# Four image layers on one core: depthwise filters cut into pieces of sixteen rows, two additions moved to VectorE, and a new planner clock

## The chip, the cores and the metric

The kernel runs on one core of a Trainium2 chip. A core has five engines that work side by side, each through its own queue of instructions in a fixed order: TensorE (PE in the profile, its weight loads PEld), VectorE (DVE), ScalarE (ACT), GpSimd (POOL), and SyncE (SP), which here issues all the DMAs. Engines wait for each other through semaphores. The metric is the time on the device in microseconds. Before the change it is 5206.15 us, the median of three runs from 5203.51 to 5209.27.

## What is computed

The input is 32 images of 56x56 pixels and 96 channels, in float32. Four layers follow each other:

```
layer 0: w = sigmoid(mean(x) @ Wr + br)              # four experts, mixed per image
         h = relu(bn(x @ sum_e w_e Wpw_e))           # 96 -> 384 channels
         h = relu(bn(depthwise3x3(h, sum_e w_e Wdw_e)))
         x = x + bn(h @ sum_e w_e Wpwl_e)            # 384 -> 96, residual
layer 1: x = x + depthwise5x5(x, kernel)
layer 2: x = bn(depthwise3x3(relu(x), dw) @ pw)      # 96 -> 96
layer 3: shifted-window attention (7x7 windows, 3 heads) with its residual,
         then x + gelu(layernorm(x) @ w1 + b1) @ w2 + b2
```

## The kernel before

**Stages and pipeline.** The work of an image is split into four stages, written as Python generators: `stage_router` (the mean and the mixed weights of layer 0), `stage_conditional` (the rest of layer 0), `stage_depthwise` (layers 1 and 2) and `stage_swin` (layer 3). In each step of the outer loop, four images are in the pipeline, each in another stage.

**Who sets the order.** The stages don't issue instructions. They record them with a `Recorder` (`chip`), with what each reads and writes. `order()` then plays the whole recording against a simple clock: `cost()` says how long each instruction holds its engine, `TO_TENSOR` and `CROSSING` how long a result takes to reach another engine, `PLAN` when each stage should begin and how long it should last in units of an image. Of the instructions that are ready, each engine takes the one that is due first. The result is a fixed list for every engine, which `give` writes out; all traced lines are therefore L500, and one goes by the names of tiles. Where this clock finds TensorE idle for over `SPARE_AFTER` = 250 ns, it inserts a filler matmul of the identity with itself (`banks<-ident 128x128`), whose result nobody uses. On the chip the lists are executed in this order, whatever the planner's clock said.

**Layer 0.** The image lies as channels by pixels in `xT`. In strips of 14 rows and blocks of 128 hidden channels, TensorE expands (`banks<-xT,wmix`), ACT writes the relu, and the 3x3 depthwise filter is one scaling on ACT and eight VectorE instructions (`h<-h,mix,h`, 128x784). The projection back (`project`) is three matmuls for seven rows (`banks<-h,wmix`), eight such groups in an image. ACT then writes scale times sum plus bias into `y`, and POOL adds `y` to `xT` (`add`).

**Layers 1 and 2.** The two depthwise filters run on TensorE as small matmuls of 32x32. The image is copied by DMA from `xT` into `x1`, where a partition holds one channel and one of four neighbouring rows (`RB` = 4), and the free dimension 14 blocks of four rows and the columns. A matmul takes 32 partitions (8 channels, 4 rows) and a banded matrix (`band5`, `band3`); because the filter crosses from one block of four rows into the next, each column offset needs two matmuls. The function `tiles` issues a step of 3 groups x 4 tiles, twelve matmuls on different parts of the array, and accumulates 10 steps (5x5) or 6 steps (3x3) in three banks. Each half of the image has its own accumulation. The first filter's result goes through ACT (relu) into `x2`, the second's through ACT into `x3` and by DMA back to channels by pixels in `filtered`; columns are turned by three for the shifted windows. Then TensorE multiplies by `pw` into `res`.

**Layer 3.** `perceptron`, at its end, has POOL add the mean that the kernel keeps in the 97th column of `res` (`tb<-res`) and then the bias `b2` (`tb<-tb,L_conv_b`), after which VectorE adds the bank of the second linear map (`tb<-banks,tb`) and SP sends `tb` to HBM.

**SP's queue.** It holds, in one order: the load of a next image (`xT<-in_x`), the 12 copies into `x1` of each image (`x<-xT`), 36 copies to `filtered`, and 8 outputs (`out<-tb`).

Of the kernel before, what the change touches and what calls it, by code (L numbers as in the profile page):

```python
# [22 lines left out]
E = 4  # L23
# [15 lines left out]
RB = 4  # L39
NBLK = H // RB  # L40
# [47 lines left out]
def banded(k, before, back):  # L88

    w = np.zeros((NQ, 8, RB, NG, 2, k.shape[2], 8, RB), np.float32)
    for q in range(NQ):
        for g in range(NG):
            first = 32 * g + 8 * ((q - g) % NQ if back else q)
            for m in range(2):
                for row in range(RB):
                    for r in range(RB):
                        dy = RB * m + row - r - before  # L100
                        if 0 <= dy < k.shape[1]:
                            for c in range(8):
                                w[q, c, row, g, m, :, c, r] = k[first + c, dy]
    return w.reshape(P, NG, 2 * k.shape[2], 32)
# [3 lines left out]
def tile_scores_in_range(ctx: ExitStack, tc: tile.TileContext, a: dict, flag: bass.AP):  # L108
# [38 lines left out]
    ("vector", "scalar_tensor_tensor"): (150, 1.16), ("vector", "tensor_tensor"): (180, 0.96),  # L147
    ("vector", "tensor_scalar"): (190, 0.78), ("vector", "tensor_reduce"): (180, 0.95),
    ("vector", "tensor_copy"): (180, 1.1), ("vector", "reciprocal"): (180, 6.2),
    ("scalar", "activation"): (200, 0.72), ("scalar", "copy"): (200, 0.72),  # L150
    ("gpsimd", "tensor_tensor"): (200, 2.1), ("gpsimd", "memset"): (150, 0),
    ("sync", "dma_start"): (550, 0),
}
LANDING = 3000
IMAGE_LANDING = 12000

PLAN = {"router": (-0.14, 1), "conditional": (0.72, 1.14), "depthwise": (1.48, 1.13), "swin": (3.09, 0.92)}
CROSSING = 350

TO_TENSOR = {"vector": 1500, "gpsimd": 1500, "scalar": 1000, "sync": 700}  # L160
SPARE_AFTER = 250
SHARING = 1.36


def cost(engine, method, args, kw):
    if method == "preload_act_table_set":
        return 1300
    out = kw["out"] if "out" in kw else args[0]
    n = math.prod(out.shape[1:])
    if engine == "tensor":  # L170
        if method == "transpose":
            return 127
        k, m = args[1].shape[0], math.prod(args[1].shape[1:])
        if k == 32 and m == 32:
            return 68 * n / 392
        if k == 32:
            return 86
        if m == 32:
            return 75 if n < 128 else 255
        return 195 if n < 128 else 80 + 1.6 * n  # L180
    if len(args) > 3 and args[3] == ALU.pow:
        return 200 + 200 * n
    fixed, each = COST[engine, method]
    if engine == "scalar":
        if kw.get("accum_out") is not None:
            fixed += 190
        if hasattr(kw.get("scale"), "shape"):
            each += 0.37 if hasattr(kw.get("bias"), "shape") else 0.23
        elif hasattr(kw.get("bias"), "shape"):
            each += 0.25  # L190
    return fixed + each * n
# [69 lines left out]
class Recorder:  # L261
# [77 lines left out]
    def order(self):  # L339
# [15 lines left out]
        for w in self.work:  # L355
            for b in w.uses:
                b.left = len(b.users)
        queues = {e: [] for e in self.ENGINES}
# [7 lines left out]
        def available(w):  # L366
            need = {}
# [6 lines left out]

        running = {}

        def share(now):

            nonlocal count
            rate = SHARING if len(running) > 1 else 1.0  # L380
            for r in running.values():
                r["left"] -= (now - r["since"]) / r["rate"]
                r["since"], r["rate"] = now, rate
                r["end"] = free[r["work"].engine] = now + max(r["left"], 0.0) * rate
                heapq.heappush(events, (r["end"], count, r))
                count += 1
# [19 lines left out]
        def begin(w):  # L406
# [9 lines left out]
            if e == "gpsimd" or e == "vector" and w.calls[0][0] == "scalar_tensor_tensor":  # L416
                running[e] = {"work": w, "left": w.ns, "since": now, "rate": 1.0}
                share(now)
                return
            free[e] = now + w.ns  # L420
            heapq.heappush(events, (free[e], count, None))
            heapq.heappush(events, (free[e] + w.landing, count + 1, w))
# [8 lines left out]
        while left:  # L431
            for e in self.ENGINES:
                if free[e] > now:
                    continue
                held = []
                while queues[e]:
                    item = heapq.heappop(queues[e])
                    w = self.work[item[1]]
                    if not available(w):
                        held.append(item)  # L440
                        continue
                    begin(w)
                    left -= 1
                    if e == "tensor":
                        spares, begun = 0, True
                    break
                else:
                    if e == "tensor" and begun and self.spare and now >= free[e] + SPARE_AFTER and self.spare[2].free:
# [5 lines left out]
                        w.ns = cost(e, "matmul", operands, {})  # L454
# [10 lines left out]
            while events and events[0][0] <= now:  # L465
# [3 lines left out]
                elif isinstance(w, dict):  # L469

                    if w["end"] == now and running.get(w["work"].engine) is w:
                        del running[w["work"].engine]
                        w["work"].end = now
                        done(w["work"], now)
                        share(now)
# [28 lines left out]
def kernel(  # L504
# [17 lines left out]
    xTs = ring("xT", [C, H * W], 2)  # L522
# [3 lines left out]
    ys = ring("y", [C, RT], 2)  # L526
# [9 lines left out]
    x3s = ring("x3", [P, NG, NBLK // 2 + 1, W], 1)  # L536
    oTs = ring("oT", [C + 1, 2 * RT], 2)
    x1s = ring("x1", [P, NG, NBLK + 1, W + 4], 1)
# [1028 lines left out]
```

## Time and profile before

| | before |
|---|---|
| median of three runs | 5206.15 us |
| span of the profiled execution | 5212.6 us |
| time from one image to the next, middle of the run | 155.0 us |
| banded matmuls (32x32), busy in all | 856.3 us, 24576 instructions |
| VectorE taps of layer 0 (`h<-h,mix,h`), busy in all | 3309.6 us, 3072 instructions |
| POOL: `xT<-y,xT` / `tb<-res`, busy in all | 470.2 us / 477.7 us |
| VectorE's last tap to the end | 285 us |

The profiled execution is one run with the profiler on; its own time is its span, 0.12% above the median. A float32 matmul of the program appears as two instructions, so 24576 instructions are 12288 matmuls. In a list in order of time, the first number is the start in microseconds from the begin of the span, the second the length of the merged group, the last the count. "Idle before" in a group's line is idle time of that engine just before the group, with what ended it.

### The profile page before, as it was taken

What the parts mean: (1) busy time and instruction counts of PE and PEld (TensorE: products, weight loads), DVE (VectorE), ACT (ScalarE), POOL (GpSimd) and SP (SyncE); (2) the same over time, 40 slices, a digit from 0 to 9 for tenths busy, and PEclk for the clock granted to TensorE, in tenths of its full rate; (3) what the DMA queues carried; (4) which work ended last, traced back from release to release, by engine and by line L of the source; (5) the groups of instructions that cost most, each with busy time, mean ns of one, the idle gap of its engine ahead of it and who ended that gap; (6) DMA issues with size and microseconds to landing.
All of it is one profiled execution on the core that took longest, in us unless ns stands there. A gap on an engine that the chain in (4) does not pass through costs nothing.

```text
span 5212.6 us, 139630 instructions
## 1 busy us (share of the span) xinstructions
PE 5050.6 (97%) x58578; PEld 3343.9 (64%) x58578; DVE 4300.9 (83%) x5561; ACT 3836.9 (74%) x7649; POOL 3028.8 (58%) x2432
## 2 busy tenths in 40 slices
PE   5789999999999999999999999999999999999999
PEld 4556666666666666666666666666666666666677
DVE  7877988888888888888888888888888888888722
ACT  3457778877778777777877777877777877777755
POOL 5455766565665556666555665656576555566533
PEclk9899999999999999999999999999999999999999
DMA  1111101111111111111111111111111111110110
GB/s 43 23 28 37 38 18 32 33 39 36 39 21 30 31 39 36 39 23 30 33 35 37 37 30 26 30 36 38 37 35 22 32 33 39 36 39 21 23 28 19
DMA packets 482577, 166.34 MB, mean 32 GB/s; under 512 B 477951, under 2 KB 478612, under 8 KB 478868
## 3 DMA queue, kind: packets, MB, share of 16 engines
q1 hardware_dynamic: 481940, 157.33, 14.8%
q8 instruction: 463, 7.59, 0.6%
q14 instruction: 174, 1.43, 0.1%
HBM read 41.60 MB, written 38.54 MB: 15 GB/s over the span
## 4 chain that ended last, share of the span: by engine, by line
PE 74%; POOL 10%; DVE 5%; ACT 5%; issue 4%; DMA 1%; SPq 0%; ACTq 0%; DVEq 0%; POOLq 0%
PE banks L500 74%; DVE h L500 3%; POOL tb L500 3%; POOL lnd L500 2%; POOL xT L500 2%; ACT exps L500 2%; POOL exps L500 2%; POOL var L500 1%; ACT hid L500 1%; ACT h L500 1%; DMA out<-tb 1%; DVE wmix L500 1%; DVE hid L500 1%; ACT slots L500 0%; DVE res L500 0%
## 5 line engine op out<-in xcount | busy, mean ns | idle before, releaser
L500 DVE SCALAR_TENSOR_TENSOR h<-h,mix,h 128x784 f32<-128x784 f32 x3072 | 3309.6, 1113 | 71.1 <-ACT h L500 54.0
L500 POOL TENSOR_TENSOR var<-var,mhalf 112x4 f32<-112x4 f32 (+1 forms) x512 | 775.2, 1519 | 426.3 <-DVE var L500 419.6
L500 PE MATMUL banks<-x,band 32*32 32x392 f32 x24576 | 856.3, 510 | 0.0
L500 POOL TENSOR_TENSOR xT<-y,xT 96x392 f32<-96x392 f32 x256 | 470.2, 1838 | 445.5 <-ACT y L500 444.1
L500 PE MATMUL banks<-xT,wmix 96*128 96x448 f32 (+1 forms) x1536 | 697.9, 553 | 0.5 <-DVE wmix L500 0.5
L500 ACT ACTIVATE h<-h,biasd,s 128x784 f32<-128x784 f32 x384 | 398.9, 1039 | 366.1 <-DVE h L500 366.0
L500 ACT ACTIVATE hid<-banks,c 128x448 f32<-128x448 f32 (+1 forms) x768 | 436.5, 582 | 288.3 <-PE banks L500 279.9
L500 POOL TENSOR_TENSOR tb<-res 112x384 f32<-112x384 f32 (+1 forms) x256 | 476.4, 1866 | 286.7 <-DMA out<-tb 196.7
L500 PEld LDWEIGHTS banks<-w,hid 128*112 128x112 f32 x5376 | 584.7, 183 | 82.0 <-issue 37.8
L500 PE MATMUL banks<-hT,w 96*128 96x448 f32 (+1 forms) x1536 | 615.6, 502 | 0.2 <-DVE tb L500 0.2
L500 POOL TENSOR_TENSOR lnd<-res,var 112x384 f32<-112x384 f32 (+1 forms) x512 | 594.8, 1168 | 32.8 <-PE banks L500 16.2
L500 ACT ACTIVATE h<-banks,bias,s 128x448 f32<-128x448 f32 (+1 forms) x768 | 538.6, 709 | 91.0 <-PE banks L500 85.4
L500 PE MATMUL banks<-w,hid 128*112 128x96 f32 x5376 | 593.1, 267 | 7.4 <-ACT hid L500 6.4
L500 PE MATMUL banks<-h,wmix 128*96 128x392 f32 x1536 | 557.7, 501 | 15.7 <-ACT h L500 15.7
L500 PEld LDWEIGHTS banks<-x,band 32*32 32x32 f32 x24576 | 404.7, 103 | 250.9 <-issue 165.9
L500 ACT ACTIVATE exps<-banks 49x196 f32<-49x196 f32 x1536 | 506.2, 330 | 40.2 <-PE banks L500 15.3
L500 POOL TENSOR_TENSOR exps<-exps,keep_column 49x147 f32<-49x147 f32 x224 | 207.1, 925 | 480.8 <-ACT exps L500 427.4
L500 PEld LDWEIGHTS banks<-h,wmix 128*96 128x96 f32 x1536 | 244.1, 165 | 256.8 <-issue 209.2
L500 PEld LDWEIGHTS banks<-xT,wmix 96*128 96x128 f32 x1536 | 261.2, 192 | 200.7 <-issue 95.5
L500 DVE TENSOR_REDUCE var<-lnsq 112x4 f32<-112x388 f32 (+1 forms) x512 | 253.1, 497 | 157.6 <-POOL lnd L500 118.1
L500 ACT ACTIVATE h<-h,mix 128x784 f32<-128x784 f32 x384 | 364.5, 949 | 18.0 <-POOL h L500 10.1
L500 PEld LDWEIGHTS banks<-hT,w 96*128 96x128 f32 x1536 | 256.4, 190 | 144.9 <-issue 74.8
(132 smaller groups left out, 7460.2 us busy)
## 6 DMA issues: line engine op xcount, KB each, us to landing
xT<-in_x SPq DMA_DIRECT2D x32, 1176.0 KB
x<-xT SPq DMA_DIRECT2D x384, 98.0 KB
out<-tb SPq DMA_DIRECT2D x128, 168.0 KB
filtered<-x SPq DMA_DIRECT2D x384, 49.0 KB
filtered<-x SPq DMA_DIRECT2D x384, 42.0 KB
out<-tb SPq DMA_DIRECT2D x128, 126.0 KB
filtered<-x SPq DMA_DIRECT2D x384, 7.0 KB
wpw<-in_L_conv_Wpw SPq DMA_DIRECT2D x1, 576.0 KB
```

What stands on the lines that cost most here:

```text
L500: getattr(getattr(self.nc, w.engine), method)(*args, **kw)
```

## The change

*Pieces of sixteen rows.* The channels are taken in three sets of 32 (`NSET`). In `x1` a partition now holds one of two channels and one of 16 rows (`BIN`), and six overlapping pieces, ten rows apart (`BOUT`), cover the image; four channel groups lie behind each other in the free dimension. Sixteen rows in give twelve after the 5x5 filter (`BMID`) and ten after the 3x3, so a filter no longer crosses from one piece to the next. `products` issues all the matmuls of one filter of one set as one unit of the order: 5 or 3 steps of 16 matmuls with 336 columns, each step on all 16 tiles of the array, into four banks. The number of matmuls per image, 384, stays. `x1` has three buffers and `x2` two. `xT` gets zero rows above and below the image. The copies into `x1` are 48 per image, each to 8 partitions (one row number of 16); those to `filtered` are 33 per image; 6 copies of zeros (`nought`) per image clear rows of `x2` outside the image. POOL repeats three columns of `x3` instead of two ACT copies per group.

*Residual of layer 0.* The scale s3 is multiplied into the expert weights once at the start. The projection's bank is added to `xT` with the bias by one VectorE instruction; `y`, its ACT instruction and POOL's add go.

*Mean of layer 3.* POOL writes `res` + `b2` into `tb` in one instruction instead of two. VectorE adds the bank, the mean (as a scalar per partition) and `tb` in one instruction per 112 pixels, seven for each pair of chunks instead of two.

*The planner's clock.* `cost` and `COST` get other constants, TensorE's time depends on the shape of its tiles, and a change of shape costs 170 ns. Among matmuls that are due at nearly the same time, one of the shape in use goes first. VectorE and POOL instructions on SBUF alone exclude each other. `PLAN`, `TO_TENSOR` and `CROSSING` change. A DMA is taken to hold SP for 120 ns, before 550.

In the written order of the whole program, fillers go from 836 to 1508 and changes of the array's tile shape from 1808 to 1031. In the even part they are 10 and 38 fillers per image.

The diff, cut to its core:

```diff
-RB = 4
-NBLK = H // RB
+NSET = 3
+NSLOT = NSET * NQ
+BIN, BMID, BOUT = 16, 12, 10
+NBLK = -(-H // BOUT)
...
-    ("sync", "dma_start"): (550, 0),
+    ("sync", "dma_start"): (120, 0),
...
-PLAN = {"router": (-0.14, 1), "conditional": (0.72, 1.14), "depthwise": (1.48, 1.13), "swin": (3.09, 0.92)}
-CROSSING = 350
-
-TO_TENSOR = {"vector": 1500, "gpsimd": 1500, "scalar": 1000, "sync": 700}
+PLAN = {"router": (-0.041, 1.106), "conditional": (0.712, 1.09), "depthwise": (1.53, 0.85), "swin": (3.09, 0.92)}
+CROSSING = 30
+
+TO_TENSOR = {"vector": 1127, "gpsimd": 2494, "scalar": 1420, "sync": 50}
 SPARE_AFTER = 250
-SHARING = 1.36
+CHANGE = 170
+SAME = 0.0315
...
+def tensor_time(calls):
+
+    rows, columns = tiling(calls[0])
+    beside = min(len(calls), (P // rows) * (P // columns))
+    if beside == 16 and len(calls) % 16:
+        beside = 12
+    total = 30 if beside > 1 else 0
+    for method, args, kw in calls:
+        m = math.prod(args[1].shape[1:])
+        n = args[1].shape[0] if method == "transpose" else math.prod(args[2].shape[1:])
+        total += 2 * ((max(n, m) if beside == 1 else n) / 1.2 + 5) / beside
+    return total
...
-    x1s = ring("x1", [P, NG, NBLK + 1, W + 4], 1)
-    x2s = ring("x2", [P, NG, NBLK + 2, W + 2], 1)
+    x1s = ring("x1", [P, NQ, NBLK, W + 4], 3)
+    x2s = ring("x2", [P, NQ, NBLK, W + 2], 2)
...
-            y = chip.new(ys)
-            chip.scalar.activation(y, pt[:C, :RT], AF.Identity, bias=bias3, scale=s3)
-            return y
+            return pt[:C, :RT]
 
         def add(n, y):
             rows = xT[:, 7 * n * W : 7 * (n + 1) * W].part(n)
-            chip.gpsimd.tensor_tensor(rows, y, rows, ALU.add)
+            chip.vector.scalar_tensor_tensor(rows, y, bias3, rows, ALU.add, ALU.add)
...
+        for u in range(NSET):
+            x1 = chip.new(x1s)
+            for r in range(BIN):
+                chip.sync.dma_start(
+                    out=lines(x1)[:, r].rearrange("c o m w -> c (o m) w")[:, :, 2 : 2 + W].part(r),
+                    in_=xT[32 * u : 32 * u + 32, r : r + BOUT * (NBLK - 1) + 1 : BOUT],
+                )
+            inputs.append(x1.part(*range(BIN)))
+            yield 2
+
+        def products(weights, src, u, dx, back):
+
+            banks = [chip.new(cv) for _ in range(NQ)]
+            with chip.together():
+                for d in range(dx):
+                    for o in range(NQ):
                         for q in range(NQ):
+                            come, go = (o, q) if back else (q, o)
+                            ks, os = slice(32 * come, 32 * come + 32), slice(32 * go, 32 * go + 32)
                             chip.tensor.matmul(
+                                banks[come][os, : NBLK * W].rearrange("p (m w) -> p m w", w=W),
+                                weights[ks, NQ * u + go, d],
+                                src[ks, go, :, d : d + W],
+                                start=(d == 0),
+                                stop=(d == dx - 1),
                             )
+            return banks
+
+        def first_filter(u):
+
+            banks = products(band5, inputs[u], u, 5, False)
...
+            for m, r in ((0, 0), (NBLK - 1, H + 1 - BOUT * (NBLK - 1))):
+                chip.sync.dma_start(
+                    out=lines(x2)[:, r, :, m, 1 : 1 + W],
+                    in_=nought.rearrange("c (o w) -> c o w", w=W),
+                )
+            return x2
...
+        waiting = []
+        for u in range(NSET):
+            waiting.append((u, first_filter(u)))
+            yield 6
+            if u > 0:
+                second_filter(*waiting.pop(0))
+                yield 4
+        second_filter(*waiting.pop(0))
+        yield 7
...
-            chip.gpsimd.tensor_tensor(tb, src[:, :, :C], src[:, :, C:].to_broadcast([LT, n, C]), ALU.add)
-            chip.gpsimd.tensor_tensor(tb, tb, b2[:LT, None, :].to_broadcast([LT, n, C]), ALU.add)
+            chip.gpsimd.tensor_tensor(tb, src[:, :, :C], b2[:LT, None, :].to_broadcast([LT, n, C]), ALU.add)
...
-            total = tb.rearrange("p j c -> p (j c)")
-            chip.vector.tensor_tensor(total, pt[:LT, : n * C], total, ALU.add)
+            for j in range(n):
+                chip.vector.scalar_tensor_tensor(
+                    tb[:, j], pt[:LT, j * C : (j + 1) * C], src[:, j, C:], tb[:, j], ALU.add, ALU.add
+                )
```

## The prediction, before the result

> **What bounds the kernel now.** I read the busy totals first, then one even stretch, then TensorE's own order of work, then SyncE's queue. The page's totals:
>
> ```profile
> PE 5050.6 (97%) x58578; PEld 3343.9 (64%) x58578; DVE 4300.9 (83%) x5561; ACT 3836.9 (74%) x7649; POOL 3028.8 (58%) x2432
> ```
>
> The table by stretches, for two images in the middle. The load of a next image (xT<-in_x) is issued at 1731.03 us, and two images later at 2041.27 us:
>
> ```profile
> 1731.00:2041.00 310.00, 306.03 (x3588) 198.99 (x3589) 268.29 (x344) 238.51 (x477) 186.10 (x150) 0.99 0.16 33
> ```
>
> Columns after the length are busy PE, PEld, DVE, ACT, POOL, the granted clock, and DMA. An image takes 155.0 us and PE is busy for 153.0 of them, DVE for 134.1, ACT for 119.3, POOL for 93.0. TensorE in its written order is the bound. Its busy time still hides short waits: adding the spacing that each kind of matmul has when nothing holds it up, over the order of one image, gives 150.1 us, so 4.9 us per image are waits.
>
> The order on TensorE (start, length), around the end of layer 0 of one image:
>
> ```profile
> 1841.25 2.14 PE L500 MATMUL banks<-h,wmix 128*96 128x392 f32 x6
> ...
> 1854.30 1.02 PE L500 MATMUL banks<-x,band 32*32 32x448 f32 x24
> 1855.25 1.03 PE L500 MATMUL banks<-pw,filtered 97*112 97x97 f32 x8
> ...
> 1885.82 0.61 PE L500 MATMUL banks<-ident 128*128 128x128 f32 x4
> 1886.36 0.86 PE L500 MATMUL banks<-exps,ones 113*32 113x392 f32 x6
> ...
> 1890.22 15.02 PE L500 MATMUL banks<-x,band 32*32 32x392 f32 x480
> 1905.17 1.02 PE L500 MATMUL banks<-xT,wmix 96*128 96x448 f32 x2
> ...
> 1919.01 0.92 PE L500 MATMUL banks<-x,band 32*32 32x392 f32 x24
> 1919.86 3.58 PE L500 MATMUL banks<-pw,filtered 97*112 97x97 f32 x34
> ```
>
> Three things are to be seen. The last projection of layer 0 is at 1841, and the first filter that needs it at 1890: there are 47 us in which the pieces can be copied. Twenty filter steps in one run take 14.95 us, 0.75 each; a step that stands alone takes 0.85 (392 columns) or 0.95 (448), so a change of the array's shape costs about 0.1. A filler (ident) costs (0.54-0.1)/2 = 0.22.
>
> SyncE's queue, where the copies into the pieces are issued (start, length, count):
>
> ```profile
> 189.69 8.23 SPq L500 DMA_DIRECT2D x<-xT  x12
> 200.20 0.34 SPq L500 DMA_DIRECT2D xT<-in_x  x1
> ```
>
> Twelve copies leave 0.69 us apart. The load behind them must wait until they have read xT: it comes 2.28 us after the last one, which is the time of a landing.
>
> **The change, part by part (us per image).**
>
> *Filters on TensorE.* Before, 32 steps of 12 tiles: 26 at 0.75 and 6 at 0.85 (448 columns cost 0.10 more), 24.6. After, 24 steps of 16 tiles and 336 columns: 0.75 less 0.10 for 56 columns fewer, plus 0.05 for four more starts in each of two passes (12 starts lie within 73 ns in the trace), 0.70; 16.8. Gain 7.8. Here a rule speaks against the change. The Trainium skill, "TensorE: Matmul & The Clock Gate", section "Wait — 56ns, not 53.3ns?", gives a floor of about 25 ns between starts however short a matmul is. The step has 32 starts, so by the rule it takes 0.80 and the gain falls to 5.4. The row's 73/11 = 6.6 ns between starts on different tiles is far below that floor, so I take the row.
>
> *Changes of shape.* The order has 1808 before and 1031 after, 24.3 fewer per image at 0.1: gain 2.4. *Fillers.* In the even part 10 per image become 38: loss 28 x 0.22 = 6.2. Both counts are of the written order, not of a clock. The fillers stand where the planner's clock left TensorE idle over 0.25 us, so it expects TensorE to wait more than before. Net of the three: -4.0, to 151.0 us per image if the other waits stay.
>
> *VectorE.* New: 8 adds of the residual 96x392 from a bank (the nearest row, a tensor_tensor of 392 columns from a bank, takes 555 ns): 4.4. New: 28 adds of 96 columns; rows at 384 and 288 columns take 551 and 451 ns, a line through them gives 0.26 at 96: 7.3. Removed: 8 adds of tb, (551+451)/2: 4.0. Net +7.7. DVE and POOL hold each other up: a layer-0 tap takes 1024 ns alone and 1113 on average, 8.5 us per image, and POOL loses about a third of the work that does it, so -3. DVE comes to 139, below 151: hidden, though with 8% of room instead of 13%.
>
> *ScalarE and GpSimd.* ACT loses 8 evacuations y (5.4) and gains 6 each of relus and copies less the small copies (about +4): level. POOL loses the adds of xT (470.2 us in all) and of tb<-res (477.7 us), 29.6 per image, and gains three short copies, under 2. Neither is near the bound; these edits I cost at nothing, hidden behind TensorE.
>
> *The hand-over from layer 0 to layer 1.* Here the sum turns. SP has 48 copies of 8x24 rows per image instead of 12, in one block, and behind them in the queue an output, the next image's load, and then the zeros for the second filter's input. All but the first two copies need the last residual add. In the new order TensorE has, between the last projection and the first filter, only 6.7 us of other work (47 before), then the second set's filter at once, and the second filter of the first set 17.9 us after the projection. SP needs: the add and its crossing 1.3; 46 copies at 0.62 (copies within SBUF of the same 192 packets take 610 ns at the median and 44 ns to the next; eight partitions instead of 32 may save some of it), 28.5; a landing, as the load waits for xT to be read, 2.3; the load 0.4; three copies of zeros 1.9; a landing 2.3: 36.7 us. TensorE stands for 36.7-17.9 = 18.8 us, in three pieces (first set, second set, zeros). Queued behind it is everything else on TensorE, and layer 0 of the next image waits for that.
>
> The price of one copy decides. Bounds: 0.37 (an output, with only one end in SBUF, 323 ns, and the gap) gives 24.4 and a stall of 6.5; 0.69, the row above, a stall of 22. The Trainium skill, "DMA: Bandwidth & Descriptors", section "Anatomy of one DMA — SWDGE (gpsimd) path", puts the sequencer's share at about 50 ns; that would end the block in 3 us, no stall, 151 per image. No SBUF copy here is near it, so I take 0.62. The same page, section "Why a DMA increments its semaphore by 16 and not by 1", says that a DMA uses only as many of 16 engines as divide both outer sizes: eight here. Each then has 24 packets, and the trace gives
>
> ```profile
> q1 hardware_dynamic: 481940, 157.33, 14.8%
> ```
>
> 0.148 x 5212.6 x 16 / 481940 = 25.6 ns for a packet of mixed sizes, so 0.61 per copy: an estimate, but it says that a faster issue would not end the block much sooner. No run here shows it yet.
>
> *Sum.* 151.0 + 18.8 = 169.8; the old waits (4.9) should vanish, since every other engine gets these 19 us of slack: 164.9. That is +9.9 in some 28 even images, +277. The ends: the last image has 107 fillers fewer (-24), cheaper filters (-8) and the stall (+19): -13. The first images wait for layer 0 alone and stay. +264 on the profiled execution's span of 5212.6, or on the median of 5206.15, which is 0.12% less: 5470. Since eight partitions may be somewhat cheaper than 32 (0.60 would take 1.0 per image), I take 5450.
>
> **Rivals.**
> *The hand-over is hidden.* The 49 copies and the 6.3 us around them end within 17.9 us if a copy costs under 0.24; then the gain stands: 151.0 x 28 instead of 155.0, -112, and the tail -32: 5060; with the old waits gone as well 146 per image, 4920. For it: TensorE, POOL and the changes of shape really lose work. Against: no SBUF copy of the trace took under 478 ns. This is the case on the other side; with the old waits gone it turns faster below 0.43 per copy, where the stall is 9.
> *The hand-over is half hidden.* Copies at 0.4, or TensorE late for other reasons inside the 17.9 us: stall 5 to 10, 151 to 157 per image, 5100 to 5290. The time before lies inside.
> *The planner was right on TensorE's idleness as well.* The gaps ahead of 38 fillers, 0.25 each, come true for VectorE's sake and add up to 5 us to the stall: 170 per image, 5600. For it: DVE rises to 139. Against: the planner lets DVE and POOL exclude each other for whole instructions.
>
> **How the numbers follow.** Stall as computed (5300 to 5560): 0.55. Worse by the planner's gaps: 0.10. Half hidden: 0.13. Hidden: 0.22. About 0.2% is what a measurement of this kernel tells from no change. Half hidden counts 0.07 slower, 0.03 same, 0.03 faster. So faster 0.25, same 0.03, slower 0.72. The likeliest case's own range is 5300 to 5560. The range reaches down to 5000 (most of the hidden case) and up to 5600.
>
> **What would show it.** Right: on SP a block of 48 copies of about 29 us per image; PE idle before banks<-x,band, released by DMA, some 15 to 19 us per image in three places; filter steps near 0.70; POOL busy down by some 900 us; DVE around 139 of 165. Wrong: a block shorter than 18 us, or no PE idle before the first filters; then the time is near 5000. A filter step over 0.8 would mean that a start has a floor.

## The result, and the profile after

The changed kernel takes 5844.61 us (median of four runs, 5841.53 to 5848.73); beside it the kernel before took 5206.23. The ratio is 1.1227, with a 95% interval of 1.1211 to 1.1243. The prediction, 5450 with a range of 5000 to 5600, had the direction and the place right and the size wrong: the loss is 638 us where it said 244.

The page's totals after, in the form in which the prediction shows those of before:

```profile
PE 5116.1 (88%) x59924; PEld 3547.0 (61%) x59924; DVE 4284.3 (73%) x6454; ACT 3792.2 (65%) x7585; POOL 2482.2 (43%) x2024
```

TensorE's share falls from 97% to 88%. The table by stretches for one image in the middle, with the same columns as before (length, then busy PE, PEld, DVE, ACT, POOL, granted clock, DMA share, GB/s):

```profile
2404.00:2581.30 177.30, 157.32 (x1856) 108.18 (x1855) 133.80 (x204) 118.28 (x237) 77.78 (x62) 0.94 0.15 34
```

An image takes 177.3 us, 155.0 before. VectorE is busy for as long as before, POOL for less, so neither is the bound. TensorE stands for 20 us of each image. Its order of time around one hand-over (start, length, count, in brackets the idle time ahead and what ended it):

```profile
2403.57 4.12 PE L538 MATMUL banks<-h,wmix 128*96 128x392 f32 x12
...
2413.84 0.55 PE L538 MATMUL banks<-ident,lnd 112*96 112x112 f32 x4
2419.23 5.81 PE L538 MATMUL banks<-x,band 32*32 32x336 f32 x160 [4.84 <-DMA x<-xT]
2429.60 5.46 PE L538 MATMUL banks<-x,band 32*32 32x336 f32 x160 [4.56 <-DMA x<-xT]
...
2439.35 0.73 PE L538 MATMUL banks<-hT,w 96*128 96x336 f32 x2
2447.85 4.25 PE L538 MATMUL banks<-x,band 32*32 32x336 f32 x96 [7.78 <-DMA x<-nought]
...
2458.33 4.09 PE L538 MATMUL banks<-x,band 32*32 32x336 f32 x160
```

The three pieces of the forecast are there, each ahead of the filter that was named: the first set, the second set, the zeros. SyncE's queue in the same stretch:

```profile
2406.39 31.64 SPq L538 DMA_DIRECT2D x<-xT  x48
2438.15 0.40 SPq L538 DMA_DIRECT2D out<-tb  x1
2439.77 0.34 SPq L538 DMA_DIRECT2D xT<-in_x  x1
2440.16 2.56 SPq L538 DMA_DIRECT2D x<-nought  x4
```

48 copies take 31.64 us, 0.66 each (forecast 0.62). The load behind them comes 1.7 us after the last copy, and the zeros right behind the load. The first 3x3 filter starts 5.1 us after the last of these four zeros was issued; the forecast gave a landing 2.3.

The filters' group (busy, mean ns of one | idle before, and what ended it), and four stretches of the clock (the granted clock is the first number after the five engines):

```profile
L538 PE MATMUL banks<-x,band 32*32 32x336 f32 x24576 | 792.4, 564 | 562.7 <-DMA x<-xT 321.2 <-DMA x<-nought 241.5
```

```profile
2419.20:2425.10 5.90, 5.81 (x160) 3.54 (x160) 3.81 (x5) 0.07 (x1) 0.00 (x0) 0.64 0.31 68
2429.60:2435.00 5.40, 5.40 (x161) 3.54 (x161) 0.00 (x0) 0.00 (x0) 0.00 (x0) 0.68 0.32 71
2447.80:2451.00 3.20, 3.15 (x82) 1.92 (x96) 0.00 (x0) 0.00 (x0) 0.00 (x0) 0.50 0.00 0
...
2458.33:2462.30 3.97, 3.97 (x161) 2.63 (x160) 3.39 (x5) 3.90 (x7) 0.98 (x1) 1.00 0.21 50
```

The idle time of 562.7 us is 17.6 per image; the forecast was 18.8. But the same five steps take 4.09 us where the clock is 1.00 and 5.5 to 5.8 right behind a stall, where it is 0.64 to 0.68 on average; behind the third stall it is 0.50. That is not in the forecast at all, and neither speed is its 0.70 per step: they are 0.82 and 1.1 to 1.2.

So the stall came nearly as reckoned, but in part by luck. From the end of the last projection (2403.57 + 4.12 = 2407.69) to the start of the first 3x3 (2447.85) pass 40.2 us, where the forecast had 36.7. The three waits in it are 17.2 us, so TensorE's own work fills 23.0, where the forecast had 17.9, since two filters run slowly there. Both terms are longer, and their difference hardly moves.

The period is 12.6 us longer than the 164.9 of the sum. The experiments look for these 12.6. A period in them is the mean distance of VectorE's first layer-0 taps of images 8 to 26: 155.3 us before, 177.5 after.

### The profile page after: what moved, and what is told of

The parts are those of the page before. It is cut to its first block, busy times and chain, and to the rows that moved or that the text cites. A ratio compares the mean times of both kernels' runs of the same rounds, so it can differ in the third digit from the quotient of the medians.

```text
span 5839.7 us, 144455 instructions
## 1 busy us (share of the span) xinstructions
PE 5116.1 (88%) x59924; PEld 3547.0 (61%) x59924; DVE 4284.3 (73%) x6454; ACT 3792.2 (65%) x7585; POOL 2482.2 (43%) x2024
## 3 DMA queue, kind: packets, MB, share of 16 engines
q8 instruction: 475, 7.78, 0.6%
## 5 line engine op out<-in xcount | busy, mean ns | idle before, releaser
L538 DVE SCALAR_TENSOR_TENSOR h<-h,mix,h 128x784 f32<-128x784 f32 x3072 | 3141.3, 1050 | 53.4 <-ACT h L538 52.2
L538 PE MATMUL banks<-x,band 32*32 32x336 f32 x24576 | 792.4, 564 | 562.7 <-DMA x<-xT 321.2
L538 DVE SCALAR_TENSOR_TENSOR tb<-banks,res,tb 112x96 f32<-112x96 f32 x896 | 273.1, 310 | 1018.5 <-PE banks L538 856.5
L538 PEld LDWEIGHTS banks<-x,band 32*32 32x32 f32 x24576 | 464.5, 116 | 855.1 <-issue 727.4
L538 POOL TENSOR_TENSOR exps<-exps,keep_column 49x147 f32<-49x147 f32 x224 | 573.2, 2564 | 834.8 <-ACT exps L538 496.3
L538 PE MATMUL banks<-xT,wmix 96*128 96x448 f32 (+1 forms) x1536 | 675.3, 544 | 25.7 <-ACT kT L538 20.7
L538 POOL TENSOR_TENSOR tb<-res,L_conv_b 112x384 f32<-112x384 f32 (+1 forms) x256 | 285.5, 1116 | 891.6 <-DMA out<-tb 724.2
L538 ACT ACTIVATE x<-banks 128x336 f32<-128x336 f32 x384 | 142.1, 458 | 596.5 <-PE banks L538 593.7
L538 PE MATMUL banks<-ident 128*128 128x128 f32 x3016 | 433.2, 287 | 34.2 <-ACT h L538 15.4
L538 PEld LDWEIGHTS banks<-ident 128*128 128x128 f32 x3016 | 388.0, 196 | 90.7 <-ACT exps L538 24.0
L538 ACT COPY x<-banks 128x336 f32<-128x336 f32 x384 | 141.2, 455 | 413.0 <-PE banks L538 409.9
```

What stands on the lines that cost most here:

```text
L538: getattr(getattr(self.nc, w.engine), method)(*args, **kw)
```

## Experiments

The theory H: the hand-over's stall and the slow clock behind it are the loss. R1: the sixteen-tile step is slow by itself. R2: the new order makes TensorE wait for other engines as well.

### A quarter of the copies

On the chip the copies with `r % 4 > 0` are not issued:

```diff
+                if w.engine == "sync" and w.skip:
+                    continue
```

> Order of all engines as in the changed kernel; of the 48 copies into x1 per image 36 are left out on the chip, so the filters read stale rows in 12 of 16 row numbers. H (the hand-over: TensorE stands 17.6 us per image for SP's copies and zeros, and its clock is halved for some 20 us after that): SP's block shrinks from 31 to 8 us, the idle time before banks<-x,band falls from 563 to under 100 us, the mean granted clock rises from 0.942 to at least 0.98, a step of 16 tiles falls from 1.03 to 0.82 us, the period from 177.3 to about 152 us, the time to about 5100. R1 (the sixteen-tile step itself is slow, by the array or the banks): the steps stay above 1.0 and the time is about 5260. R2 (the new order makes TensorE wait for other engines as well): the idle time comes back elsewhere, and the time stays above 5500.

5179.7 us, ratio to before 0.9962 (0.9947 to 0.9978), against 1.1227 with all copies. That is 80 us more than H expected. TensorE's group of the filters, and of two others:

```profile
L541 PE MATMUL banks<-x,band 32*32 32x336 f32 x24576 | 649.2, 457 | 38.7 <-issue 33.4 <-DMA x<-xT 4.2 <-DMA x<-nought 0.9
L541 PE MATMUL banks<-xT,wmix 96*128 96x448 f32 (+1 forms) x1536 | 676.5, 545 | 25.7 <-ACT kT L541 20.7 <-DVE wmix L541 5.0
L541 PE MATMUL banks<-exps,ones 113*32 113x392 f32 x1536 | 220.7, 505 | 39.4 <-POOL exps L541 39.0 <-ACT x L541 0.4
```

The same two others in the changed kernel:

```profile
L538 PE MATMUL banks<-xT,wmix 96*128 96x448 f32 (+1 forms) x1536 | 675.3, 544 | 25.7 <-ACT kT L538 20.7 <-DVE wmix L538 5.0
L538 PE MATMUL banks<-exps,ones 113*32 113x392 f32 x1536 | 220.0, 503 | 39.6 <-POOL exps L538 39.2 <-ACT x L538 0.4
```

665 us hang on 36 of 48 copies, in an unchanged order: the hand-over is the loss. By the rows they are 524 us of idle time before the filters (562.7 less 38.7) and 143 us of slower filters (792.4 less 649.2). R1 falls: the five steps take 4.09 us here, 0.82 each. R2 falls too as the cause of the difference. But the rows of the two other groups show something the forecast had wrong. TensorE's waits there are the same to 0.2 us with the hand-over and without. They did not vanish behind 20 us of stall: one is for exps out of GpSimd, one for kT out of ScalarE, and the stall comes elsewhere in the image.

They are not the waits of the kernel before either. There the largest stood in front of `banks<-ident,lnd`, and exps had almost none (two lines of before, one of the changed kernel):

```profile
L500 PE MATMUL banks<-ident,lnd 112*96 112x112 f32 x1792 | 258.0, 265 | 51.3 <-POOL lnd L500 51.3
L500 PE MATMUL banks<-exps,ones 113*32 113x392 f32 x1536 | 221.7, 505 | 1.1 <-POOL exps L500 1.1
...
L538 PE MATMUL banks<-ident,lnd 112*96 112x112 f32 x1792 | 254.9, 261 | 0.6 <-ACT slots L538 0.6
```

So the new order removed the old wait and brought others, and the stall removed none of these. The period without the hand-over is 156.2, not 151.0 and still less 146.

### The stall kept, the clock kept full

Fillers are issued directly ahead of the three filters that wait, into the bank that the filter then begins anew (`WARM` is 20, 18 and 30):

```diff
+                for _ in range(w.warm):
+                    bank = w.writes[0].ring.tiles[w.writes[0].slot]
+                    self.nc.tensor.matmul(bank[:, :P], self.spare[0], self.spare[1], start=True, stop=True)
```

> All copies stay. 68 more fillers per image (identity by identity, 0.22 us each) stand directly before the three filters that wait: 20 before the first set's 5x5, 18 before the second's, 30 before the first 3x3. They need no copy, and end before it has landed: 4.4, 4.0 and 6.6 us inside waits of 4.84, 4.56 and 7.78. H: the waits end at the same time, but TensorE is at full clock after them: the clock of the records rises to about 0.99, the filters' busy time falls from 792 to about 640 us, and the period by 5 us for the filters and some 3 us for the other matmuls after the waits: about 5590 (5560 to 5650). R1: steps stay at 1.03 to 1.15 us with a full clock, and the time is 5840 or more. If the low clock came from power and not from standing still, it would stay at 0.94.

5813.4 us, 1.1177 (1.1155 to 1.12). The granted clock is 0.984, and the filters' busy time falls as expected:

```profile
L543 PE MATMUL banks<-x,band 32*32 32x336 f32 x24576 | 680.1, 479 | 161.0 <-DMA x<-xT 76.0 <-DMA x<-nought 74.3 <-issue 10.4
```

Yet the period falls by 1.2 us, not by 8. H's second half was wrong. The last projection and the first 3x3 of one image:

```profile
2386.02 4.11 PE L543 MATMUL banks<-h,wmix 128*96 128x392 f32 x12
...
2430.24 2.52 PE L543 MATMUL banks<-x,band 32*32 32x336 f32 x96 [1.76 <-DMA x<-nought]
```

From the end of the one to the start of the other pass 40.1 us, as in the changed kernel (40.2). A slow first filter only fills time in which the next copies are still being issued: a filter that ends earlier waits longer. Only what follows the last wait gains: this 3x3 takes 2.52 us instead of 4.25. The clock costs little here because the copies and zeros set the end.

The halved rate is what the Trainium skill describes ("TensorE: Matmul & The Clock Gate", section "Part 1: The HAM clock gate (the "warmup" mystery)"): after an idle window of about 3.4 us TensorE runs at half rate until it has been busy for as long. All three stalls, 4.6 to 7.8 us, are longer than that, and the 0.50 above agrees, as do the 0.64 and 0.68, which are means over a slow and a full part. What it costs is another matter: by the filters' rows (143 us) the slow steps are 4.5 us per image, and undoing them gained 1.2.

### Old planner, new planner, additions: the other corners

Two runs exchange the planner whole (`cost`, `COST`, `PLAN`, the landing and crossing times and the `Recorder`): the changed kernel with the old one, the kernel before with the new one. Two put the additions into the kernel before, with s3 multiplied into the weights, under the old planner and under the new. The core of these edits:

```diff
-            chip.gpsimd.tensor_tensor(rows, y, rows, ALU.add)
+            chip.vector.scalar_tensor_tensor(rows, y, bias3, rows, ALU.add, ALU.add)
...
-            chip.vector.tensor_tensor(total, pt[:LT, : n * C], total, ALU.add)
+            for j in range(n):
+                chip.vector.scalar_tensor_tensor(
+                    tb[:, j], pt[:LT, j * C : (j + 1) * C], src[:, j, C:], tb[:, j], ALU.add, ALU.add
+                )
```

> The changed kernel's filters and additions, ordered with the planner, costs and due times of before (a DMA holds SP for 550 ns, PLAN and crossing times of before). In its written order the first filter stands 18 us of other work behind the last projection (5.7 in the changed kernel), and the first 3x3 35 us (17.9). SP needs about 14 us for the first set, 23 for the second, 37 for the zeros. H: at most 3 us of stall per image, clock above 0.98, a period of 152 to 158 us, 5100 to 5300. R1 gives some 5 us per image more, about 5400. If the filters' copies cost by loading the DMA queue and not by the order, the time stays above 5600.

> The kernel before, filters, additions and all, ordered with the new planner (costs, due times, shape rule, a DMA at 120 ns). H: with 12 copies of 0.69 us per image in place of 48 the hand-over is 9 us and not 31, so little of the loss appears: within 2% of 5206. R2 (the new order is bad of itself): 5400 or more.

> The kernel before, its filters and its planner, with only the two additions moved to VectorE. The prediction costs them at nothing: VectorE at 139 of 155 us. But the order changes with them: 1222 fillers against 836, 12 per image, which at 0.22 us would be 2.7 us per image if none stands in a wait. Expected 5150 to 5300. If VectorE or the path from the bank to xT became the bound: above 5350.

> The kernel before with the two VectorE additions and the new planner, without the new filters. The old planner with the additions took 5663 us, the new planner without them 5415. If the new planner's clock suits the additions (it doesn't take an addition from a bank as sharing with GpSimd), the time is 5150 to 5300, period 153 to 158; the rest of the change, the filters, is then the whole loss. If additions and planner each cost what they cost alone, 5414 + 459 = about 5870.

| filters | additions | planner | us | ratio to before (95%) | period |
|---|---|---|---|---|---|
| old | POOL | old | 5206 | 1 | 155.3 |
| old | POOL | new | 5415 | 1.0413 (1.0396 to 1.0431) | 163.2 |
| old | VectorE | old | 5663 | 1.0893 (1.0860 to 1.0925) | 171.8 |
| old | VectorE | new | 5206 | 0.9994 (0.9985 to 1.0003) | 157.1 |
| new | VectorE | old | 5416 | 1.0402 (1.0384 to 1.0420) | 164.3 |
| new | VectorE | new | 5845 | 1.1227 (1.1211 to 1.1243) | 177.5 |

Planner and additions alone each lose hundreds of microseconds, together nothing. Of the four expectations the last was met in full; the first missed by 116 us, the other two by 105 and 363. The first and second landed on the numbers of R1 (about 5400) and R2 (5400 or more). R1's cause does not hold in the first: five steps at full clock take 4.09 us there too. R2 does hold in the second, for the old filters with POOL's additions: TensorE stands 113.8 us for exps there, 1.1 before. In the worst of them, the additions with the old planner, TensorE waits at one place above all:

```profile
L500 PE MATMUL banks<-ident,lnd 112*96 112x112 f32 x1792 | 268.3, 270 | 219.2 <-POOL lnd L500 218.8
```

Before, this idle time was 51.3 us, with the new planner it is 19.5. The work on VectorE is the same 4.3 ms with the additions under either planner, so it is the order and not the additions. That the old planner treats an addition from a bank as one that shares memory with GpSimd, and so spreads the work wrongly, may be why; that was not tried alone.

The fourth line is the one that counts: with additions and planner in place and the old filters, the time is that of before. All of the 638 us comes when the filters and their copies join this planner. It is not the filters by themselves: in the old planner's order they make the kernel with the additions faster, 5416 instead of 5663. The new filters with POOL's additions were not run under either planner.

And the filters bring little even without their copies: a period of 157.1 falls to 156.2 in the run with a quarter of them, where the forecast had TensorE gain 7.8. The gain itself is there. The old filters' group in the fourth run:

```profile
L536 PE MATMUL banks<-x,band 32*32 32x392 f32 x24576 | 869.4, 513 | 0.7 <-issue 0.7
```

Against the 649.2 us of the run with a quarter of the copies this is 6.9 us more per image. But the time is filled again: the fillers' rows are 244.6 us in the fourth run and 429.2 in the other, 5.8 more per image.

The first line of new filters says where the copies' cost sits. In the old planner's order the first filter stands 18 us behind the last projection and does not wait, but the second set's does (3.0 to 5.6 us) and the first 3x3 (4.1 to 6.2): idle before the filters is 293.8 us, half of the 562.7.

### A DMA at its real price in the planner

```diff
-    ("sync", "dma_start"): (120, 0),
+    ("sync", "dma_start"): (640, 0),
```

> The changed kernel with one number of the planner's clock altered: a DMA holds SP for 640 ns, not 120. In the written order the first 5x5 then stands 13 us of other TensorE work behind the last projection, the second 25, the first 3x3 38 us (5.7, 5.7 plus a filter, and 17.9 in the changed kernel). SP needs some 14, 24 and 41 us. H (the loss is the order's, which thinks SP five times too fast): stall under 4 us per image, period 155 to 158 us, time 5190 to 5290. Rival (the copies cost as much wherever the filters stand, or the new planner's other waits decide): 5400 or more.

5352.3 us, 1.0287 (1.0270 to 1.0305), period 161.7: one number of the planner, with the order that follows from it, is worth 492 us, 77% of the loss. The stall is as expected (104.9 us, 3.3 per image), the period 4 us above the expected band. Of the stall 81 us is one thing:

```profile
2537.88 4.09 PE L538 MATMUL banks<-x,band 32*32 32x336 f32 x160
2556.09 3.83 PE L538 MATMUL banks<-x,band 32*32 32x336 f32 x96 [3.47 <-DMA x<-nought]
```

```profile
2545.94 1.32 SPq L538 DMA_DIRECT2D x<-nought  x2
2547.37 0.89 SPq L538 DMA_DIRECT2D out<-tb  x2
2548.42 0.40 SPq L538 DMA_DIRECT2D xT<-in_x  x1
2548.87 1.28 SPq L538 DMA_DIRECT2D x<-nought  x2
```

The first 3x3 needs one of the two zeros behind the image load, and starts 7.2 us after SP began to issue them.

### The zeros ahead of the image load

The load of a next image is held back on the chip until the next four zeros are issued, in the second run, which has the DMA at 640 ns as well, the next two:

```diff
+                if w.load and w.start > 3e5:
+                    held, zeros = w, 0
+                    continue
...
+                    if zeros == 4:
+                        method, args, kw = held.calls[0]
...
+                        self.nc.sync.dma_start(**kw)
```

> Order as in the changed kernel, but on SP the load of a next image is issued behind the next four copies of zeros, not ahead of them. In the changed kernel the last zero is issued at 2442.7 us and the first 3x3 starts at 2447.85, 5.1 us later, while the image load fills the DMA engines. H: the zeros wait in the DMA engines for the load's 1.2 MB; ahead of it they land 2 to 3 us after their issue, the idle time by x<-nought falls from 241 to under 80 us, the period from 177.4 by 5 to 7 us, the time to about 5650 (5610 to 5700). Rival: 5 us is what such a copy takes; then only its 0.4 us earlier issue counts and the time stays above 5800.

> Both repairs: a DMA at 640 ns in the planner's clock, and the image load behind the next two copies of zeros. The run with the price alone took 5352 us, with 105 us of idle time before the filters, 81 of them until zeros had landed. H: these 81 us go, and the clock stays full after the first 3x3 begins: 5352 - 81 - 30 = about 5240. If the load of the image, now later, is what layer 0 then waits for, it is no faster than 5352.

The first: 5647.0 us, 1.0849 (1.0827 to 1.0872), period 170.6, 7.0 less than the changed kernel. The second: 5235.0 us, 1.0060 (1.0043 to 1.0077), period 156.9. Both as expected. SyncE and TensorE in the first:

```profile
2505.90 32.33 SPq L543 DMA_DIRECT2D x<-xT  x48
2538.84 2.63 SPq L543 DMA_DIRECT2D x<-nought  x4
2541.65 0.34 SPq L549 DMA_DIRECT2D xT<-in_x  x1
```

```profile
2529.72 6.55 PE L543 MATMUL banks<-x,band 32*32 32x336 f32 x160 [5.43 <-DMA x<-xT]
2542.15 2.52 PE L543 MATMUL banks<-x,band 32*32 32x336 f32 x96 [0.87 <-DMA x<-nought]
```

The filter waits 0.87 us here instead of 7.78; over the run the idle time by `x<-nought` is 72.4 us instead of 241.5. The changed kernel's trace shows why. Between 2440.3 and 2445.3 us, while four zeros of 224-byte packets were issued, the DMA engines moved the image alone:

```profile
DMA packets 89, 1.12 MB, mean 223 GB/s; under 512 B 0, under 2 KB 0, under 8 KB 0
```

So 7 KB of zeros were late because 1.2 MB stood ahead of them. The filters in the first and in the second run:

```profile
L543 PE MATMUL banks<-x,band 32*32 32x336 f32 x24576 | 773.6, 550 | 392.3 <-DMA x<-xT 318.9 <-DMA x<-nought 72.4 <-issue 0.8
...
L543 PE MATMUL banks<-x,band 32*32 32x336 f32 x24576 | 649.9, 457 | 29.5 <-DMA x<-xT 15.4 <-issue 12.7 <-ACT h L543 1.0
```

With both repairs 0.9 us per image is left before the filters, and the kernel is 0.6% slower than before. It is the best complete version found here, and not faster than before.

### Two queues for the copies

Every second copy into `x1` is issued from ScalarE's queue, at its place in the order:

```diff
-                    getattr(getattr(self.nc, w.engine), method)(*args, **kw)
+                    getattr(getattr(self.nc, w.through or w.engine), method)(*args, **kw)
...
+                chip.work[-1].through = "scalar" if r % 2 else None
```

> Order as in the changed kernel; every second copy into x1 is issued by ScalarE, the others by SP. If the 0.62 us of a copy is the time of the issuing queue alone, each queue has 24 copies, the block is 16 us and not 31, the stall falls from 17.6 to about 4 us per image and the time to about 5400. If the DMA engines behind the queue set it (24 packets each at 25.6 ns is 0.61 us too), the last copy lands no earlier, both queues take 1.2 us per copy, and the time stays at 5840.

5553.5 us, 1.0669 (1.0648 to 1.0691): between the two. SyncE's half of the block, and a part of ScalarE's:

```profile
2454.96 22.76 SPq L539 DMA_DIRECT2D x<-xT  x24
2463.17 7.54 ACTq L539 DMA_DIRECT2D x<-xT  x8
2470.76 0.68 ACT L539 ACTIVATE h<-banks,bias,s 128x392 f32<-128x392 f32 x1 [7.17 <-DMA x<-xT]
```

24 copies take 22.8 us on SP, while ScalarE issues the other 24; the last of these ends at 2479.1, 24.2 us after the first. That is 0.50 per copy for both together; it was 0.66 for SP alone, and would be 0.33 if the queue were everything. So about half of the price is the queue's own, and something behind the queues is shared. The DMA engines are a candidate, not shown: their share over the block is 0.29 of sixteen engines in the changed kernel and 0.52 to 0.57 here. The prediction's estimate that a faster issue would not end the block much sooner does not hold: 31.6 us became 24.2. The time gains less than the block, also because ScalarE's own work now stands behind its copies (7.2 us in the last line), and TensorE waits 64 us for ScalarE before the filters.

SP's issues in the changed kernel (least, median and most ns of one):

```profile
L538 SPq DMA_DIRECT2D x<-xT x1536: 597/597/1962, 151.3 to 5623.3; - x192
L538 SPq DMA_DIRECT2D x<-nought x192: 597/619/852, 185.2 to 5640.6; - x192
```

A copy of zeros has 32 packets and one into x1 has 192; SP spends 0.60 to 0.62 us on either, so the price does not go by packets.

### Without the fillers

The run with a quarter of the copies, and no filler issued:

```diff
-                if w.engine == "sync" and w.skip:
+                if w.engine == "sync" and w.skip or w.spare:
                     continue
```

> The run with a quarter of the copies (which leaves 36 of 48 copies per image out, and took 5180 us at a period of 154), without the fillers: 38 per image fewer. If each costs TensorE 0.22 us, as the prediction reckoned, the period falls by up to 8.4 us and the time to about 4920. If they stand where TensorE waits anyway, the time stays within 1% of 5180, and the same waits show as idle time of TensorE. If fillers are needed for the clock, the granted clock falls below 0.98 and the time rises.

5383.3 us, 1.0342 (1.0322 to 1.0363): 204 us slower than with them, at a granted clock of 0.926 instead of 0.989. The page's totals without fillers, then with them, and the fillers' row of the latter:

```profile
PE 4939.8 (92%) x56908; PEld 3298.7 (61%) x56908; DVE 4298.1 (80%) x6454; ACT 3788.6 (70%) x7585; POOL 2567.3 (48%) x2024
...
PE 4967.1 (96%) x59924; PEld 3493.6 (68%) x59924; DVE 4299.2 (83%) x6454; ACT 3786.2 (73%) x7585; POOL 2522.2 (49%) x2024
...
L541 PE MATMUL banks<-ident 128*128 128x128 f32 x3016 | 429.2, 286 | 33.0 <-ACT h L541 16.0 <-ACT exps L541 12.3 <-DVE xT L541 4.3
```

The forecast charged each filler 0.22 us, 6.2 per image more than before. Taken out, they save nothing, and the third expectation is the one that came. By the totals and the spans (5376.6 and 5175.7 us), 429 us of fillers go; TensorE is idle 228 us more, and all its other matmuls are busy 402 us longer, at the lower clock. So at least about half of the fillers' time was time in which TensorE waits anyway. Whether the rest would be saved at an unchanged clock no run shows.

### Half the columns

```diff
+                    if w.half:
+                        args[0], args[2] = args[0][:, :3], args[2][:, :3]
```

> The run with a quarter of the copies (36 of 48 left out), and every filter matmul computes 168 of its 336 columns (three of six pieces; the other half of the outputs is left as it was). Order as in the changed kernel. If a step of 16 tiles is set by its 32 starts (25.6 ns each, 0.82 us), a run of five steps still takes 4.0 to 4.1 us at full clock. If columns set it (1.8 ns per column by the rows of before, 392 columns at 0.75 and 448 at 0.85), five steps take 2 to 2.5 us.

5120.4 us (one run). Two runs of filters, at 168 columns and, from the run with a quarter of the copies, at 336:

```profile
2755.33 1.69 PE L543 MATMUL banks<-x,band 32*32 32x168 f32 x96
2762.23 2.66 PE L543 MATMUL banks<-x,band 32*32 32x168 f32 x160
```

```profile
2315.71 2.53 PE L541 MATMUL banks<-x,band 32*32 32x336 f32 x96
2323.44 4.09 PE L541 MATMUL banks<-x,band 32*32 32x336 f32 x160
```

Five steps less three are two: 0.485 us per step at 168 columns, 0.78 at 336 (0.82 with the run's end shared out). With 32 starts in a step that is 15.2 ns per start in the first. The floor of about 25 ns that the prediction weighed (the Trainium skill, "TensorE: Matmul & The Clock Gate", section "Wait — 56ns, not 53.3ns?") is therefore not what sets 0.78, close as 0.80 is. Columns do at least in part: 168 of them cost 0.295 us, 1.76 ns each, close to the slope that the rows of before give (0.10 for 56). If that is a line, the new thing is an offset: by that slope a step of 12 tiles had 0.06 us besides its columns, one of 16 has 0.19. Behind the first pass of a run most single starts are 15 to 18 ns apart, in both kernels, with longer pauses between; the 6.6 ns of the forecast are those of the first pass. So at 168 columns the starts, at 15.2 ns each, may already set the step, and two widths don't tell this from a line. Why 16 tiles at 336 columns cost 0.13 more than the line through 12 was not found.

And the time: TensorE does 6.6 us less filter work per image (649.2 - 438.3 = 210.9 us in all), and the period falls by 1.5, from 156.2 to 154.7. With the hand-over gone, in this order, a microsecond saved on TensorE is not a microsecond of the period.

## Why the prediction was right, and where not

*Right: the place and the mechanism.* SP's block of 48 copies, three stalls ahead of the filters named, 0.66 per copy (0.62), VectorE hidden (134 of 177; 139 of 165 forecast). The 17.6 us of stall per image (18.8 forecast) are in part luck, as said: the stretch from projection to 3x3 and TensorE's work in it were both longer. The run with a quarter of the copies shows that this is the whole loss. The 50 ns per copy that the prediction also weighed belong, by the title of the section it names, to the path through GpSimd; SyncE issues these copies, so it was no bound for them. The rival *hidden* fell with the copy's price: it needed less than 0.24. That the additions cost nothing was right, but only together with the new planner.

*Wrong: "the old waits (4.9) should vanish".* This is the largest single term that failed, 4.9 us per image. The stall removed no wait: the rows of exps (39.6 and 39.4 us) and the waits for kT (20.7 both) are the same with and without the hand-over. The old wait for lnd did go (51.3 to 0.6), but with the new order, with or without the stall, and others came. A likely reason is that slack of the other engines removes a wait only if the wait is for their throughput, and these are for one result at one place; no run shows that.

*Wrong: the landing of the zeros.* 2.3 was taken from a copy with nothing ahead of it. Behind the image load it is 5.1 from the last of the four, and the order of the two is worth 7.0 us per image. The forecast listed the load ahead of the zeros and charged it 0.4, its issue.

*Wrong: 0.70 for a step.* It measured 0.82 at full clock; 24 x 0.12 = 2.9 per image. The failed step is the choice of the 73 ns burst for the spacing of starts; the rule's number would have been nearer, but not for its reason, since with half the columns a start came every 15.2 ns.

*Missing: the clock behind a stall.* 1.2 us per image, less than the 4.5 of its rows.

*Wrong: "the first images wait for layer 0 alone".* The first eight images lose 137 us (image 8 begins its taps at 1342 us, before at 1205), 17 each. At 22.3 per image the whole loss is that of nearly 30 images, less 28 us at the end (VectorE's last tap to the end: 285 us before, 257 after); the sum had 28 images.

*The sum.* The 12.6 us by which the period exceeds the 164.9 are three parts. Without the hand-over it is 156.2 and not 151.0: 5.2, of which 2.9 is the step; the rest was not split. The 4.9 that should have vanished is the second. The hand-over is 177.5 - 156.2 = 21.3 and not 18.8: 2.5. In this last part the zeros' landing adds 2.8 and the clock behind the last stall 1.2, while slower filters inside the block take some back, since they fill time that would be waited for.

*VectorE and GpSimd.* The line through 551 and 451 ns gives 0.25 us for an addition of 96 columns, not 0.26; the rows measured 0.31, hidden all the same. POOL is busy for 547 us less and not for 900: the row of its exps with keep_column took 573.2 us instead of 207.1, which the forecast left as it was. Whether TensorE's wait for exps (39.6 us, 1.1 before) comes from that was not tried.

*Fillers.* The count of 38 was read as a sign that the planner expects TensorE to wait, and each was charged 0.22 besides. At least about half of their time did stand in waits. Taking them out gained nothing, so the charge was wrong as a price of these fillers at the clock that they keep.

*The range.* It ended at 5600 because the worst case added gaps to the stall but still let the old waits vanish. With them kept, and the zeros at 5, it would have reached 5600 + 28 x (4.9 + 2.8), about 5800, still short of 5845.

## What to carry to other kernels

When a planner writes the order, its price of one instruction is part of the kernel: 120 ns for a DMA that takes SP 660 cost 492 us here. Judge each part of such a change in the order it will run in, since planner and additions lost 209 and 457 us apart and nothing together, and with the additions in place the filters gained 247 us under one planner and lost 639 under the other. A stall need not swallow waits that stand elsewhere in the period, and a small transfer that someone waits for belongs ahead of a large one in the same queue.

## What was not expected of the hardware

A DMA within SBUF costs SP's queue 0.60 us for 192 packets and 0.62 for 32. The same copies issued from two queues take 0.50 us each and not half of 0.66. Leaving the fillers out cost 204 us, at a granted clock of 0.926 instead of 0.989 in an otherwise equal order. A half-rate clock behind a stall costs 1.2 us per image, and not the 4.5 of the slower rows, since most of it falls inside the next wait. Steps of 16 tiles of 32x32 with 336 columns take 0.13 us more than the line through steps of 12.
